# Sort comparisons by whole piece and chunk comparisons by whole load in a graph layer's scatter-add

## The chip, the cores and the metric

The kernel runs on one NeuronCore of one Trainium2 chip. The metric is device time in microseconds (us) of one execution. The core has five engines with a queue each: PE (TensorE, matrix products), DVE (VectorE), ACT (ScalarE), POOL (GpSimd, which here issues the indirect transfers) and SP (SyncE, which issues direct transfers). Each engine takes its instructions strictly in the order in which they stand in the program; an instruction that waits holds up all behind it on the same engine.

## The reference

`x` has 6250 nodes of 128 features, `edge_attr_128` has 206,250 edges of 128 features, and `src` names the node of each edge. What is computed:

```python
edge_aggr = zeros(n, 128).at[src].add(edge_attr_128)         # scatter-add of the edges
combined  = concat([x, edge_aggr, global_expand]) @ W_c + b_c
h = softplus(combined @ W1 + b1)
h = softplus(h @ W2 + b2)
out = layernorm(x + h @ W3 + b3)
```

Nearly all of the time goes into the scatter-add.

## The kernel before, in words

The nodes are cut into 32 **buckets** of 196 nodes. The edges lie in 1692 columns of 122 edges; two columns are a **pair** (846 pairs), three pairs a **piece** (`PAIRS`, 286 pieces with the short ones), and the pieces are cut into 8 groups. The scatter-add runs in three stages that overlap from beginning to end:

1. **Positions.** For each group `positions` works out, on DVE and PE by turns, at which place of its bucket each edge goes (DVE tiles `pair_ib`, `past`, `slot`, `pair` and many small ones). The result for sorting is `slot`: the place of each edge inside its column.
2. **Sort and scatter.** For each piece: *compare* makes 0/1 matrices (`sort_hot`, one 122x128 matrix for each column) out of `slot`; *gather* multiplies them on PE with the loaded edge rows, so that a column's rows come out sorted (`sorted`, three columns to a PSUM bank); *settle* copies them on ACT into one of six sets (`pairs`, line 1165); and POOL issues one indirect transfer for each pair (line 1182, `rows_by<-pairs,pair`), 846 in all, which puts the rows into their buckets in memory (`rows_by`).
3. **Chunks.** Rows come back bucket by bucket as **chunks** of 128 rows (1758 of them) in **loads** of at most eight chunks (`LOAD_CHUNKS`, 301 loads). *match* (line 983, DVE) compares the node of each row with the 196 nodes of the bucket (`hot`, 128x196 for each chunk), *product* (line 1006, PE) multiplies the chunk with that matrix and adds up in PSUM (`part`), and *add* (line 1029, DVE) adds a finished part to `sums_t`.

A piece has two **units**: its three even columns and its three odd ones. Before, the even unit is compared on DVE in one instruction over 3x128 elements (line 1133), and the odd unit on ACT, with three Abs instructions over 128 elements (line 1140) and one Relu over 384 (line 1142). A load's chunks are cut into units of at most `HALF` = 4 chunks: one match and one run of products each, 512 units in all.

The order on PE, DVE, ACT and SP is written out by a planner: every step is given a due time with `when(t, step)`, all steps are sorted by it, and each engine's instructions are issued in that order. The due times come from a model in which a pair is scattered every `SCATTER` = 1.3; for a piece that is scattered from t on, the compare is due at t - `COMPARED`, the gather at t - `GATHERED` and the settle at t - `SETTLED`. The due times are not times on the chip: they only set the order. In `sum_steps` a match is due no earlier than the product of the unit `TOGETHER` = 2 before it (`AT_END` before it, after the last scatter), and a load no earlier than the product that frees its buffer.

When the last pair is scattered, the steps left over are handed as `rest` to `node_layers`, which works through the chunks that remain and, as soon as the sums of a tile of nodes are there, runs the dense layers, the softplus and the layer norm on it: at each step up to `FIRST_STEPS` of the left-over steps, then the second and third products, then the rest that the next tile needs.

## Time and profile before

Times and the profiled execution:

| | |
|---|---|
| median of 3 runs | 1299.63 us (1296.0 to 1299.84) |
| the profiled execution's own time | 1298.25 us |
| its span, first to last instruction | 1296.5 us |
| mean granted TensorE clock | 0.963 |
| busy PE / DVE / ACT / POOL | 1169.6 / 1073.4 / 1064.2 / 877.7 us |
| scatters (POOL) | 846, the first issued at 23.4 us, the last at 1132.4 us |

What lies between the span and the profiled execution's time is 1.75 us. A row of a group of instructions names line, engine and operation, the tiles (out<-in), the shape, the count, then the busy time, the mean of one in ns, and the engine's idle time just before them with what ended it. A row of the timeline begins with the start in us and the duration; "x2" there is two instructions that follow each other without a gap, and what stands in brackets is the idle time before them and what ended it. A TensorE product of 32-bit numbers appears as two MATMULs and two weight loads, so 162 MATMULs on line 1006 are 81 chunks.

### The profile page before, as it was taken

The numbers are of one execution on the slowest core, as the hardware profiler recorded it, in microseconds if no ns is written. First come the engines' busy times: TensorE is split into PE (matmuls) and PEld (weight loads), VectorE is DVE, ScalarE is ACT, GpSimd is POOL, SyncE is SP. The second block draws the span as 40 slices with busy tenths as digits, with TensorE's granted clock in tenths as the row PEclk, the third lists the DMA queues.
The fourth block names the chain that finished last, engine by engine and source line by source line (L and its number), as shares of the span: only waits on it lengthen the run. The fifth ranks groups of instructions, "written<-read, shape, count | busy, mean of one in ns | idle before, by whom it ended". The sixth has DMA issues, their size and how long they took to land.

```text
span 1296.5 us, 26618 instructions
## 1 busy us (share of the span) xinstructions
PE 1169.6 (90%) x8617; PEld 1108.0 (85%) x8617; DVE 1073.4 (83%) x2403; ACT 1064.2 (82%) x2484; POOL 877.7 (68%) x915
## 2 busy tenths in 40 slices
PE   5767898878999998999899999999999999999893
PEld 4657788877998898998799999999999999998762
DVE  7968988998899988899878887799877666687784
ACT  5998998899978898987999999998999999504353
POOL 2777777777776677776777777777777777740334
PEclk9888998989999899999999999999999999999996
DMA  6789998899999998996989999999999999874421
GB/s 227 245 273 346 344 326 305 305 337 369 364 321 316 362 329 295 311 316 238 314 296 306 325 332 321 355 294 325 337 348 336 361 340 353 279 220 144 142 77 52
DMA packets 174638, 381.99 MB, mean 295 GB/s; under 512 B 27546, under 2 KB 118626, under 8 KB 160670
## 3 DMA queue, kind: packets, MB, share of 16 engines
q1 hardware_dynamic: 130751, 260.70, 60.4%
q0 software_dynamic: 41328, 115.65, 23.0%
q10 hardware_dynamic: 2415, 3.87, 0.8%
q8 instruction: 72, 1.18, 0.4%
q14 instruction: 72, 0.59, 0.1%
HBM read 242.49 MB, written 142.20 MB: 297 GB/s over the span
## 4 chain that ended last, share of the span: by engine, by line
PE 42%; DVE 21%; DMA 15%; ACT 9%; issue 7%; POOL 6%; SPq 0%; ACTq 0%; DVEq 0%; POOLq 0%
PE part L1006 24%; PE sorted L1153 13%; DMA rows_by<-pairs,pair 11%; POOL rows_by L1182 6%; ACT pairs L1165 6%; DVE hot L983 4%; DMA chunks<-rows_by 3%; ACT sort_hot L1140 2%; DVE sort_hot L1133 2%; DVE pair_ib L491 2%; DVE past L720 2%; DVE sums_t L1029 2%; DVE slot L569 1%; PE small L1383 1%; DMA rows<-in_edge 1%
## 5 line engine op out<-in xcount | busy, mean ns | idle before, releaser
L1182 POOL DMA_INDIRECT rows_by<-pairs,pair x846 | 824.8, 975 | 306.9 <-issue 204.5
L1006 PE MATMUL part<-hot,chunks 128*128 128x196 f32 x3516 | 674.1, 335 | 12.2 <-DVE sums_t L1029 9.2
L1165 ACT COPY pairs<-sorted 64x387 f32<-64x387 f32 (+2 forms) x1144 | 542.7, 474 | 70.0 <-PE sorted L1153 49.5
L1006 PEld LDWEIGHTS part<-hot,chunks 128*128 128x128 f32 x3516 | 581.1, 192 | 21.2 <-DVE sums_t L1029 10.3
L1153 PE MATMUL sorted<-rows,sort_hot 122*128 122x129 f32 x3384 | 497.4, 287 | 43.3 <-ACT pairs L1165 37.2
L1153 PEld LDWEIGHTS sorted<-rows,sort_hot 122*128 122x128 f32 x3384 | 454.0, 198 | 55.6 <-ACT pairs L1165 51.8
L983 DVE TENSOR_TENSOR hot<-chunks,both_ps 128x784 f32<-128x784 f32 (+3 forms) x541 | 427.9, 810 | 5.6 <-DMA chunks<-rows_by 5.2
L1140 ACT ACTIVATE sort_hot<-plain,slot 122x128 f32<-122x128 f32 x846 | 278.3, 391 | 13.1 <-DVE slot L569 7.1
L1029 DVE TENSOR_TENSOR sums_t<-sums_t,part 128x392 f32<-128x392 f32 (+1 forms) x262 | 143.5, 548 | 117.4 <-PE part L1006 116.7
L1142 ACT ACTIVATE sort_hot<-sort_hot,ones 122x384 f32<-122x384 f32 (+2 forms) x286 | 174.6, 611 | 9.3
L1133 DVE TENSOR_TENSOR sort_hot<-slot,both_ps 122x384 f32<-122x384 f32 (+2 forms) x286 | 154.5, 541 | 3.2 <-PE sorted L1153 3.0
L491 DVE TENSOR_TENSOR pair_ib<-pair_block,both_ps 122x512 bf16<-122x512 bf16 (+2 forms) x157 | 103.5, 664 | 0.3
L1425 POOL TENSOR_SCALAR y<-y,mv,rs 128x128 f32<-128x128 f32 x40 | 31.1, 785 | 96.9 <-issue 67.7
L569 DVE TENSOR_REDUCE slot<-small 122x16 f32<-122x512 f32 (+2 forms) x109 | 72.8, 668 | 15.3 <-PE small L552 14.8
L1355 ACT ACTIVATE away<-sorted,z_bias 128x512 f32<-128x512 f32 (+2 forms) x13 | 8.5, 656 | 70.8 <-DMA chunks<-rows_by 46.3
L550 PE MATMUL small<-pair_ib,half 122*122 122x512 bf16 (+2 forms) x109 | 43.0, 395 | 10.0 <-DVE slot L569 9.6
L735 PEld LDWEIGHTS <-past 128*128 128x128 f16 x424 | 24.9, 99 | 17.9 <-DVE past L720 12.6
L720 DVE TENSOR_TENSOR past<-both_ps,starts 128x512 f16<-128x512 f32 (+1 forms) x61 | 40.0, 666 | 0.3
L735 PE MATMUL small<-jump,past 128*128 128x56 f16 (+3 forms) x424 | 29.2, 190 | 11.5 <-DVE past L720 8.1
L1107 ACT COPY rows<-pair_i 122x16 f32<-122x16 f32 x106 | 22.6, 213 | 17.8 <-DMA rows<-in_edge 16.9
L552 PEld LDWEIGHTS <-starts_h 128*122 128x122 bf16 x236 | 24.9, 146 | 12.1 <-issue 7.6
L720 DVE TENSOR_TENSOR past<-both_ps,starts_late 128x512 f16<-128x512 f32 (+2 forms) x49 | 32.3, 661 | 0.0
(163 smaller groups left out, 520.0 us busy)
## 6 DMA issues: line engine op xcount, KB each, us to landing
rows<-in_edge SPq DMA_DIRECT2D x105, 1032.0 KB
chunks<-rows_by SPq DMA_DIRECT2D x362, 136.0 KB
chunks<-rows_by SPq DMA_DIRECT2D x203, 204.0 KB
chunks<-rows_by SPq DMA_DIRECT2D x75, 272.0 KB
rows_by<-pairs,pair POOLq DMA_INDIRECT x846
rows_by<-fill SPq DMA_DIRECT2D x10, 1249.5 KB
rows_by<-fill SPq DMA_DIRECT2D x10, 714.0 KB
chunks<-rows_by SPq DMA_DIRECT2D x13, 408.0 KB
```

Of the source, the lines that this page charges most:

```text
L491: nc.vector.tensor_tensor(ib, pair_block[:, cols].unsqueeze(2).to_broadcast([PN, n, SB]), iota_ps[:PN, :SB].unsqueeze(1).to_broadcast([PN, ...
L569: nc.vector.tensor_reduce(to, of, axis=mybir.AxisListType.X, op=ALU.max)
L720: nc.vector.tensor_tensor(past[:, :, a:b], twice_ps[:KB].unsqueeze(1).unsqueeze(1).to_broadcast([KB, 2, b - a, P // 2]), own["starts"][:, ...
L983: nc.vector.tensor_tensor(hot[:, q - a:q - a + m], chunks[j][:, lo:hi + 1:step, D:W].to_broadcast([P, m, BL]), iota_ps.unsqueeze(1).to_bro ...
L1006: nc.tensor.matmul(part[:, b - base_of[v], :], t[:, place_in(j, q), :D], hot[:, q - a], start=first, stop=last)
L1029: nc.vector.tensor_add(here, here, of)
L1133: nc.vector.tensor_tensor(hot[:PN, :m], slot[:PN, at:at + 2 * m - 1:2].unsqueeze(2).to_broadcast([PN, m, P]), slot_ps[:PN].unsqueeze(1).to ...
L1140: nc.scalar.activation(hot[:PN, j], by_slot[:PN], AF.Abs, bias=slot[:PN, at:at + 1], scale=-1.0)
L1142: nc.scalar.activation(hot[:PN, :m], hot[:PN, :m], AF.Relu, bias=ones[:PN, :1], scale=-1.0)
L1153: nc.tensor.matmul(out[:, j, :], hot[:PN, j], rows_at[col // LOAD_COLS][:PN, col % LOAD_COLS, :], start=True, stop=True)
L1165: nc.scalar.copy(sets_at[i][64 * n:64 * n + 64, lo:lo + m, h, :W], out[64 * h:64 * h + 64, :m, :])
L1182: s = nc.gpsimd.indirect_dma_start(out=dst, out_offset=bass.IndirectOffsetOnAxis(ap=at, axis=0), in_=rows[:, j].rearrange("p a b -> p (a b ...
```

## The change

It has four parts.

- **Sort comparisons by piece.** `compare` takes a whole piece, six columns. Even pieces are compared on DVE, in one instruction over 6x128 elements; odd pieces on ACT, in six Abs over 128 elements and one Relu over 768. On ACT the seven instructions are seven steps with due times of their own, 0.65 apart (`SCATTER` / 2) and beginning `SPREAD` = 2.0 earlier, so that settles of earlier pieces come to stand between them. The tile `sort_hot` is twice as large, and there are three in place of five.
- **Chunks by whole load.** `HALF` goes from 4 to 8: a load is one unit. There are 301 units in place of 512; three `hot` tiles of eight chunks stand in place of six of four.
- **The end.** `AT_END` goes from 4 to 2 units and `FIRST_STEPS` from 9 to 5 steps.
- The bias of the Relu and of the logarithm is the constant 1.0 in place of a column of the tile `ones`.

```diff
-HALF = 4
+HALF = 8
...
-SHARE = 2
+SHARE, SPREAD = 2, 2.0
 PREP, LAG = 0.85, 11.0
 TOGETHER, BEHIND = 2, 1
-AT_END, FIRST_STEPS = 4, 9
+AT_END, FIRST_STEPS = 2, 5
...
-    hots = ctx.enter_context(tc.tile_pool(name="hots", bufs=6))
+    hots = ctx.enter_context(tc.tile_pool(name="hots", bufs=3))
...
-        sort_p = phase.enter_context(tc.tile_pool(name="sort", bufs=5))
+        sort_p = phase.enter_context(tc.tile_pool(name="sort", bufs=3))
...
-        def compare(unit):
-            i, lo, m, n = unit
-            g, c, _ = pieces[i]
-            slot = slot_of[g]
...
-            hot = sort_p.tile([P, THREE, P], F32, name="sort_hot")
-            hot_of[unit] = hot
-            if (2 * i + n) % SHARE == 0:
-                at = 2 * (c - groups[g][0] + lo) + n
-                nc.vector.tensor_tensor(
-                    hot[:PN, :m],
-                    slot[:PN, at:at + 2 * m - 1:2].unsqueeze(2).to_broadcast([PN, m, P]),
-                    slot_ps[:PN].unsqueeze(1).to_broadcast([PN, m, P]), op=ALU.is_equal)
-                return
-            for j in range(m):
-                at = 2 * (c - groups[g][0] + lo + j) + n
-                nc.scalar.activation(hot[:PN, j], by_slot[:PN], AF.Abs,
-                                     bias=slot[:PN, at:at + 1], scale=-1.0)
-            nc.scalar.activation(hot[:PN, :m], hot[:PN, :m], AF.Relu, bias=ones[:PN, :1],
-                                 scale=-1.0)
+        def compare(i):
+            g, c, m = pieces[i]
+            slot, at = slot_of[g], 2 * (c - groups[g][0])
...
+            hot = hot_of[i] = sort_p.tile([P, 2 * PAIRS, P], F32, name="sort_hot")
+            if i % SHARE == 0:
+                return [lambda: nc.vector.tensor_tensor(
+                    hot[:PN, :2 * m], slot[:PN, at:at + 2 * m].unsqueeze(2).to_broadcast([PN, 2 * m, P]),
+                    slot_ps[:PN].unsqueeze(1).to_broadcast([PN, 2 * m, P]), op=ALU.is_equal)]
+            return [lambda j=j: nc.scalar.activation(
+                hot[:PN, j], by_slot[:PN], AF.Abs, bias=slot[:PN, at + j:at + j + 1], scale=-1.0)
+                for j in range(2 * m)] + [lambda: nc.scalar.activation(
+                    hot[:PN, :2 * m], hot[:PN, :2 * m], AF.Relu, bias=1.0, scale=-1.0)]
...
-                nc.tensor.matmul(out[:, j, :], hot[:PN, j],
+                nc.tensor.matmul(out[:, j, :], hot[:PN, at],
...
+            comparing = {}
+
+            def compare_next(i):
+                if i not in comparing:
+                    comparing[i] = compare(i)
+                comparing[i].pop(0)()
+
             for i, t in enumerate(begins):
                 mine = units(i)
+                soon = 0.0 if i else SOON
+                if i % SHARE == 0:
+                    when(t - COMPARED - soon, lambda i=i: compare_next(i))
+                else:
+                    for j in range(2 * pieces[i][2] + 1):
+                        when(t - COMPARED - SPREAD + j * SCATTER / 2, lambda i=i: compare_next(i))
                 for u, unit in enumerate(mine):
...
-                    when(t - COMPARED + late_by - soon, lambda unit=unit: compare(unit))
...
-            nc.scalar.activation(away[:, :w], away[:, :w], AF.Ln, bias=ones[:, :1])
+            nc.scalar.activation(away[:, :w], away[:, :w], AF.Ln, bias=1.0)
```

In the built program the DVE instructions of line 983 go from 541 to 346, the DVE sort comparisons from 286 to 143, the Relus from 286 to 143 and the Abs from 846 to 840; PE's products, the copies, the scatters and all transfers keep their number.

Three places show how the order moves. The first is DVE while the second half of the sixth group's positions is made (`pair_ib`, `past`, `slot`); before:

```order
L1029 TENSOR_TENSOR sums_t<-sums_t,part 128x392
L983 TENSOR_TENSOR hot<-chunks,both_ps 128x588
L1133 TENSOR_TENSOR sort_hot<-slot,both_ps 122x384
L491 TENSOR_TENSOR pair_ib<-pair_block,both_ps 122x512
L983 TENSOR_TENSOR hot<-chunks,both_ps 128x588
L720 TENSOR_TENSOR past<-both_ps,starts_late 128x512
L569 TENSOR_REDUCE slot<-small 122x2x2x4
```

and with the change:

```order
L1029 TENSOR_TENSOR sums_t<-sums_t,part 128x392
L983 TENSOR_TENSOR hot<-chunks,both_ps 128x1176
L1130 TENSOR_TENSOR sort_hot<-slot,both_ps 122x768
L491 TENSOR_TENSOR pair_ib<-pair_block,both_ps 122x512
L693 TENSOR_TENSOR earlier_late<-earlier_late 128x64
L696 SCALAR_TENSOR_TENSOR far<-plain 128x1
```

Two matches of three chunks have become one of six, and the sort comparison is twice as wide; in the next cycle of DVE, not shown, there is none.

The second place is ACT in the middle of the program; `pairs_112` and `pairs_113` are the sets of two pieces that follow each other. Before:

```order
L1140 ACTIVATE sort_hot<-plain,slot 122x128 x3
L1142 ACTIVATE sort_hot<-sort_hot,ones 122x384
L1165 COPY pairs_112<-sorted 64x3x129 x4
L1140 ACTIVATE sort_hot<-plain,slot 122x128 x3
L1142 ACTIVATE sort_hot<-sort_hot,ones 122x384
L1165 COPY pairs_113<-sorted 64x3x129 x4
```

and with the change:

```order
L1158 COPY pairs_112<-sorted 64x3x129 x4
L1133 ACTIVATE sort_hot<-plain,slot 122x128 x2
L1158 COPY pairs_113<-sorted 64x3x129 x2
L1133 ACTIVATE sort_hot<-plain,slot 122x128 x3
L1158 COPY pairs_113<-sorted 64x3x129 x2
L1133 ACTIVATE sort_hot<-plain,slot 122x128
L1135 ACTIVATE sort_hot<-sort_hot 122x768
```

The comparison of one odd piece now stands between the copies of two pieces, and the four copies of the second of them are split by three Abs.

The third place is PE in the last group, between gathers (line 1153, now 1146) and products (line 1006). Before:

```order
L1153 MATMUL sorted<-rows,sort_hot 128x129 x3
L1006 MATMUL part<-hot,chunks 128x196 x3
L1153 MATMUL sorted<-rows,sort_hot 128x129 x3
L1006 MATMUL part<-hot,chunks 128x196 x3
L1153 MATMUL sorted<-rows,sort_hot 128x129 x3
```

and with the change:

```order
L1146 MATMUL sorted<-rows,sort_hot 128x129 x3
L1006 MATMUL part<-hot,chunks 128x196 x6
L1146 MATMUL sorted<-rows,sort_hot 128x129 x6
L1006 MATMUL part<-hot,chunks 128x196 x6
L1146 MATMUL sorted<-rows,sort_hot 128x129 x6
```

Gathers of three columns and products of three chunks used to alternate; now both units of a piece are gathered in one go, and a whole load is multiplied in one go.

More of the change, by code (lines that the diff above doesn't have):

```diff
@@ L1122 @@
         hot_of, sorted_of = {}, {}
[L1124 to L1143 removed]
+        def compare(i):
+            g, c, m = pieces[i]
+            slot, at = slot_of[g], 2 * (c - groups[g][0])
+            assert all((g, at + j) in slots_done for j in range(2 * m))
+            hot = hot_of[i] = sort_p.tile([P, 2 * PAIRS, P], F32, name="sort_hot")
[7 more added lines that the diff above has]
+                    hot[:PN, :2 * m], hot[:PN, :2 * m], AF.Relu, bias=1.0, scale=-1.0)]
         def gather(unit):
             i, lo, m, n = unit
[L1147 removed]
+            hot = hot_of[i]
             out = opened_bank(lambda: settle(unit))
```

2 lines of the change are left out of this document (removed).

## The prediction

> **What bounds the kernel now.** I read the scatters first, since everything after them waits for the last one. This is line 1182 by itself, and two rows of POOL's timeline in a quiet place:
>
> ```profile
> L1182 POOL DMA_INDIRECT rows_by<-pairs,pair x846: 971/972/1222, 23.4 to 1132.4; - x170
> ...
> 1000.81 0.97 POOL L1182 DMA_INDIRECT rows_by<-pairs,pair  x1 [0.30 <-issue]
> 1002.09 0.97 POOL L1182 DMA_INDIRECT rows_by<-pairs,pair  x1 [0.30 <-issue]
> ```
>
> Undisturbed, a scatter starts 1.28 us after the one before (1002.09 - 1000.81; 0.97 busy and 0.30 of issue). 845 such steps are about 1080 us; from 23.4 to 1132.4 the kernel took 1109. So only some **29 us** of the scatter stage are lateness; nothing in the change touches the 1.28. Where they lie is seen by stage, with the busy time and count of each engine:
>
> ```profile
> core 0: us, PE busy (x) PEld busy (x) DVE busy (x) ACT busy (x) POOL busy (x), PEclk, DMA share, GB/s
> 120.00:320.00 200.00, 171.63 (x1373) 160.66 (x1372) 176.78 (x433) 181.04 (x429) 149.50 (x154) 0.94 0.91 325
> 320.00:640.00 320.00, 296.97 (x2340) 285.95 (x2339) 292.66 (x677) 278.12 (x658) 228.42 (x235) 0.97 0.90 317
> 640.00:1120.00 480.00, 474.50 (x3478) 467.53 (x3477) 377.51 (x671) 450.02 (x1064) 363.21 (x374) 0.99 0.94 326
> 1133.00:1297.00 164.00, 132.01 (x672) 110.41 (x672) 119.14 (x286) 55.21 (x95) 52.19 (x65) 0.92 0.43 129
> ...
> 565.00:621.00 56.00, 50.67 (x401) 47.70 (x400) 55.49 (x128) 44.23 (x106) 37.76 (x40) 0.97 0.80 287
> ```
>
> From 320 to 640 POOL issued 235 scatters, 300 us' worth, in 320: **about 20 of the 29 us** are there, 3 between 120 and 320 (154 are 197), about 1 after 640 (374 are 478). What POOL and the engines behind it waited for from 320 to 640 (total us, times, longest):
>
> ```profile
> ACT pairs L1165 <- PE sorted L1153: 21.0, 24, 2.6
> POOL rows_by L1182 <- ACT pairs L1165: 18.8, 19, 3.6
> ACT rows L1107 <- DMA rows<-in_edge: 10.9, 4, 3.9
> POOL rows_by L1182 <- DMA rows_by<-pairs,pair: 8.9, 19, 1.9
> DVE z_bias L1079 <- PE small L1078: 4.8, 1, 4.8
> ```
>
> POOL waits for ACT's copies, ACT for PE's gathers, and PE for DVE, as the timeline of DVE in the fullest stretch shows (565 to 621, DVE busy 55.49 of 56 us):
>
> ```profile
> 577.64 0.75 DVE L983 TENSOR_TENSOR hot<-chunks,both_ps 128x588 f32<-128x588 f32 x1
> 578.32 0.54 DVE L1133 TENSOR_TENSOR sort_hot<-slot,both_ps 122x384 f32<-122x384 f32 x1
> 578.78 0.68 DVE L491 TENSOR_TENSOR pair_ib<-pair_block,both_ps 122x512 bf16<-122x512 bf16 x1
> ...
> 582.40 0.54 DVE L1133 TENSOR_TENSOR sort_hot<-slot,both_ps 122x384 f32<-122x384 f32 x1
> ...
> 585.81 0.96 DVE L983 TENSOR_TENSOR hot<-chunks,both_ps 128x784 f32<-128x784 f32 x1
> 586.69 0.54 DVE L1133 TENSOR_TENSOR sort_hot<-slot,both_ps 122x384 f32<-122x384 f32 x1
> ```
>
> There is one `sort_hot` per piece, so DVE's cycle is 582.40 - 578.32 = **4.08 us a piece**, against 3 x 1.28 = 3.83 for its three scatters: 0.25 us late with every piece. DVE leads in such stretches; elsewhere in 320 to 640 it is transfers (the third to fifth rows of the waits). From 640 on PE is busy 474.5 of 480 us while POOL keeps its pace, so there a faster DVE or ACT buys nothing.
>
> **The change, part by part. DVE's merged comparisons.** The matches fall from 541 to 346 instructions, the sort comparisons from 286 to 143; the elements stay. A merge saves what an instruction costs beside its elements. By duration:
>
> ```profile
> L983 DVE TENSOR_TENSOR hot<-chunks,both_ps 128x784 f32<-128x784 f32 x230 | 218.9, 963 | 5.3 <-DMA chunks<-rows_by 5.0
> L983 DVE TENSOR_TENSOR hot<-chunks,both_ps 128x588 f32<-128x588 f32 x223 | 166.7, 759 | 0.3 <-DMA chunks<-rows_by 0.2
> L983 DVE TENSOR_TENSOR hot<-chunks,both_ps 128x392 f32<-128x392 f32 x81 | 42.6, 554 | 0.0
> ```
>
> 784 - 392 elements cost 409 ns, 1.04 ns each; 588 x 1.04 = 612, and 759 - 612 leaves **0.147 us** fixed. But from start to start the 588 above took 578.32 - 577.64 = 0.68 us and the 784 took 0.88: 588 x 1.04 leaves **0.068**, 784 leaves 0.065. The next instruction begins before the last has ended, so in a stretch without gaps a merge saves 0.065. I take 0.065, since only full stretches matter, and keep 0.147 as the upper end. In all 338 merges are 22 us of DVE (50 by duration), most of it where DVE has time anyway. [...]
>
> In the full stretch two pieces lose three instructions (two matches of three become one of six twice, two sort comparisons become one): 3 x 0.065 = 0.195 us, **0.10 a piece of the 0.25 that are late**, two fifths. If all 20 us of 320 to 640 were DVE's that is 8 us; with the 10.9, 8.9 (of which 19 x 0.30 are ordinary issue) and 4.8 us of transfer and PE waits in it, I take 0.4 x 15 = **-6**. Bounds: 0 (PE busy 297 of 320 does not let it through) and 0.147 x 3 / 2 = 0.22 a piece, 0.88 x 20 = -17.6.
>
> **ACT.** Its parts, by shape:
>
> ```profile
> L1165 ACT COPY pairs<-sorted 64x387 f32<-64x387 f32 x1116 | 534.5, 479 | 68.0 <-PE sorted L1153 48.0 <-PE small L552 0.2 <-DMA rows_by<-pairs,pair 0.2
> L1140 ACT ACTIVATE sort_hot<-plain,slot 122x128 f32<-122x128 f32 x846 | 278.3, 391 | 13.1 <-DVE slot L569 7.1
> L1142 ACT ACTIVATE sort_hot<-sort_hot,ones 122x384 f32<-122x384 f32 x279 | 171.6, 615 | 9.0
> L1142 ACT ACTIVATE sort_hot<-sort_hot,ones 122x128 f32<-122x128 f32 x5 | 2.0, 401 | 0.2
> ```
>
> Two pieces take 8 x 0.479 + 6 x 0.391 + 2 x 0.615 = 7.41 us of the 7.67 in which they are scattered: ACT is nearly full and, once late, regains 0.26 per two pieces. The Relu costs (615 - 401) / 256 = 0.84 ns an element and 0.29 fixed, so one over 768 elements is 0.94 in place of 1.23: 7.12, and it regains 0.55, twice as fast. This can only shorten lateness that outlasts its cause; the 3 us of 120 to 320 and what is left of 320 to 640 are of that kind. I take **-1.5** (0 to -5). Moving the steps costs nothing by itself: between the last copies of an even and of an odd piece ACT now has two Abs, two copies, three Abs, two copies, 5 x 0.391 + 4 x 0.479 = 3.87 us, and from there to the next even piece one Abs, the Relu and four copies, 3.25; 3.87 is 0.04 over the pace. If the copies lead by less than that, it is 0.04 once.
>
> **Start.** The first piece is compared on DVE as a whole: 384 elements more, 0.40 us, ahead of the first gather. I take **+0.4** (0 to 0.4; its odd half leaves ACT).
>
> **After the last scatter.** PE does the chunks that are left and the dense layers, and is held up in places:
>
> ```profile
> 1134.94 0.97 DVE L983 TENSOR_TENSOR hot<-chunks,both_ps 128x784 f32<-128x784 f32 x1 [2.52 <-DMA chunks<-rows_by]
> ...
> 1136.44 28.81 PE L1006 MATMUL part<-hot,chunks 128*128 128x196 f32 x162 [3.51 <-DVE sums_t L1029]
> ...
> 1202.28 1.56 PE L1006 MATMUL part<-hot,chunks 128*128 128x196 f32 x8 [1.68 <-issue]
> ...
> 1218.79 1.59 PE L1006 MATMUL part<-hot,chunks 128*128 128x196 f32 x8 [1.02 <-DVE sums_t L1029]
> ...
> 1246.65 1.59 PE L1006 MATMUL part<-hot,chunks 128*128 128x196 f32 x8 [1.22 <-DVE sums_t L1029]
> ```
>
> The 3.51 us are the wait for the last rows: the load lands, DVE compares four chunks (0.97), adds, and PE goes on. Eight chunks are 4 x 196 x 1.04 = 0.82 us more, on the path: **+0.8**. From the last sort comparison on 93 matches become 64, which spares DVE 29 x 0.065 = 1.9 us (4.3 at 0.147), and DVE is what the other rows wait for; against it a match of 1.7 us can stand ahead of an add. `AT_END` halved over units twice as long keeps the same look-ahead in chunks, and five steps for nine likewise. I take **-1.0** (-4 to +4). A trade that the stretch of DVE decides either way.
>
> The bias of 1.0 is an operand in another place: nothing, since no instruction is added. Three `hot` tiles of eight hold as many chunks as six of four, but a load of two chunks takes a whole one; where DVE is ahead of PE, in the 640 to 1120 in which it is busy only 377.51 of 480 us, a wait for a tile costs nothing that the wait of an add for the same products does not: 0, or, where DVE leads, a part of the bound of 0 for its gain.
>
> **Sum:** -6 - 1.5 + 0.4 + 0.8 - 1.0 = **-7.3 us**. From the profiled execution's 1298.25 that is 1291.0. The median of the runs, 1299.63, lies 0.1% above that execution, within their spread of 3.8 us; I stay with **1291**.
>
> **The rivals.** *The whole fixed cost comes back.* If every merge in the full stretches spares 0.147 us, 0.22 of the 0.25 a piece go, 17.6 us in place of 6, and the lateness ends almost wholly: 1298.25 - 17.6 - 1.3 = 1279. For it: the rows by duration; against it: the starts. [...] Chance 0.12.
>
> *No change.* PE decides. It is busy 297 of 320 us before 640 and without a gap after, and its work is the same. To end 7 us sooner it must lose 7 of the 23 idle us in that stage; if these are its waits for loads (10.9 us on ACT's side) and not for DVE, POOL's gain is eaten by PE's, and 1296 to 1301 comes out. For it: 474.5 of 480; against it: in the full stretch, 565 to 621, the waits run from PE to DVE. Chance 0.24.
>
> *Slower: longer runs of products ahead of the gathers.* PE now runs six to eight chunks in one go where three or four stood between two gathers. A chunk is 28.81 / 81 = 0.36 us, so a gather behind it can come 3 x 0.36 = 1.07 us later, and its copies and scatters too, where nothing is in hand. Over the whole run:
>
> ```profile
> POOL rows_by L1182 <- ACT pairs L1165: 30.0, 40, 3.6
> ```
>
> 40 times POOL already waits for the copies. If the longer run comes on top at 15 of them, that is +16, with the -7.3 about 1307; it decides from about 11 places on (11 x 1.07 = 11.8, the gain and 0.3%). Against it: both units of a piece are now gathered together, so the wait comes once a piece. Chance 0.16.
>
> **How the numbers follow.** Below 0.3%, 3.9 us, this kernel's measurement can't tell a change. The forecast has 0.48, by itself 1285 to 1295.7; with the first rival, faster is 0.60; the same 0.24; slower 0.16. The range takes in the bound of 17.6 us for DVE with a little more from ACT, 1277, and of the slower case what lies near, 1303: beyond them I leave about 0.06 and 0.13.
>
> **What would show it.** Right: the matches of 1568 elements take 1.78 us (0.147 + 1.63) and the sort comparisons of 768 take 0.95; the Relu 0.94; the last scatter starts near 1125 in place of 1132; the scatters from 320 to 640 rise from 235 to about 240; in the full stretch DVE's cycle falls to about 8.0 us for two pieces; POOL's waits for ACT's copies fall. The time from the last scatter to the end stays within 3 us of 164. Wrong: POOL's waits for copies grow, or the gathers wait for the Relu (the slower case); the last scatter comes sooner but the tail grows by as much (PE decides); or DVE begins to wait at line 983 for PE, which means that three tiles are too few.

## The result: 0.5% slower, and the profile after

The changed kernel takes 1304.12 us (median of 12 executions, 1302.13 to 1311.17), the kernel before, measured beside it, 1298.91 (12 executions, 1296.0 to 1300.53). The ratio is **1.0052, 95% interval 1.0035 to 1.0068**: 5.2 us slower, where 1291 had been forecast with a range up to 1303. The profiled execution took 1303.65 us with a span of 1301.9.

The page and the view of the scatters' line show that the work per engine fell as it should, and that the scatters nevertheless ended later:

```profile
PE 1168.6 (90%) x8617; PEld 1111.4 (85%) x8617; DVE 1051.6 (81%) x2065; ACT 1003.2 (77%) x2335; POOL 878.9 (68%) x915
```

```profile
L1175 POOL DMA_INDIRECT rows_by<-pairs,pair x846: 971/972/1417, 23.5 to 1137.6; - x170
```

DVE is busy 22 us less than before, ACT 61 us less. The first scatter starts at 23.5 (before 23.4), the last at 1137.6 (before 1132.4). From there to the end are 1301.9 - 1137.6 = 164.3 us (before 1296.5 - 1132.4 = 164.1). So in these two profiles the whole loss lies between the first and the last scatter, and the two constants of the end have hardly a part in it. By stage (columns as in the same view of before):

```profile
120.00:320.00 200.00, 170.42 (x1387) 160.28 (x1387) 176.83 (x398) 171.98 (x406) 150.08 (x153) 0.96 0.92 326
320.00:640.00 320.00, 291.67 (x2280) 282.73 (x2280) 279.69 (x562) 253.84 (x597) 224.75 (x230) 0.95 0.89 311
640.00:1120.00 480.00, 474.97 (x3492) 469.16 (x3491) 371.44 (x520) 427.09 (x1005) 364.35 (x375) 1.00 0.95 327
```

From 120 to 320 and from 640 on the count of scatters is within one of what it was. From 320 to 640 POOL issued 230 in place of 235, 5 x 1.28 = 6.4 us' worth less, although DVE was busy 13 us less there. Part of that is the five scatters that are missing; for each scatter DVE was busy 279.69 / 230 = 1.216 us in place of 292.66 / 235 = 1.245, which is 6.9 us over 235. **DVE's saving is there, and the scatters did not get it.** The waits that answer to those of the prediction, over the whole run:

```profile
ACT pairs L1158 <- PE sorted L1146: 122.8, 125, 6.2
...
POOL rows_by L1175 <- ACT pairs L1158: 44.0, 64, 4.9
...
PE sorted L1146 <- ACT sort_hot L1135: 25.9, 19, 2.2
...
DVE hot L983 <- PE part L1006: 9.6, 11, 2.2
```

POOL's waits for the copies grew from 30.0 us in 40 to 44.0 in 64, and the longest from 3.6 to 4.9. Gathers now wait for the Relu (25.9 us), and DVE for a `hot` tile (9.6 us). These are the signs that the prediction named for being wrong: longer waits for copies, gathers that wait for the Relu, DVE that waits for a tile. ACT's wait for gathers, 122.8 us where it was 49.5, is no such sign: with the sort part alone, which does not lose (next section), it is 109.7.

### The profile page after: what moved, and what is told of

It is laid out like the page before. It is cut to its first block, busy times and chain, and to the rows that moved or that the text cites. A ratio compares the mean times of both kernels' runs of the same rounds, so it can differ in the third digit from the quotient of the medians.

```text
span 1301.9 us, 26116 instructions
## 1 busy us (share of the span) xinstructions
PE 1168.6 (90%) x8617; PEld 1111.4 (85%) x8617; DVE 1051.6 (81%) x2065; ACT 1003.2 (77%) x2335; POOL 878.9 (68%) x915
## 4 chain that ended last, share of the span: by engine, by line
PE 58%; DVE 19%; DMA 11%; ACT 7%; issue 4%; POOL 1%; SPq 0%; DVEq 0%; ACTq 0%; POOLq 0%
PE part L1006 34%; PE sorted L1146 18%; DMA chunks<-rows_by 5%; DVE hot L983 4%; ACT pairs L1158 4%; DMA rows_by<-pairs,pair 3%; ACT sort_hot L1133 2%; DVE pair_ib L491 2%; DVE sort_hot L1130 2%; DVE slot L569 2%; DVE past L720 1%; DMA rows<-in_edge 1%; DVE sums_t L1029 1%; PE small L550 1%; PE small L552 1%
## 5 line engine op out<-in xcount | busy, mean ns | idle before, releaser
L1006 PE MATMUL part<-hot,chunks 128*128 128x196 f32 x3516 | 648.4, 336 | 21.6 <-DVE sums_t L1029 10.5
L1158 ACT COPY pairs<-sorted 64x387 f32<-64x387 f32 (+2 forms) x1144 | 542.6, 474 | 141.7 <-PE sorted L1146 122.8
L1006 PEld LDWEIGHTS part<-hot,chunks 128*128 128x128 f32 x3516 | 588.7, 193 | 32.2 <-DVE sums_t L1029 12.2
L1146 PE MATMUL sorted<-rows,sort_hot 122*128 122x129 f32 x3384 | 479.0, 286 | 42.2 <-ACT sort_hot L1135 25.9
L1146 PEld LDWEIGHTS sorted<-rows,sort_hot 122*128 122x128 f32 x3384 | 438.1, 197 | 51.2 <-ACT sort_hot L1135 29.5
L983 DVE TENSOR_TENSOR hot<-chunks,both_ps 128x1568 f32<-128x1568 f32 (+7 forms) x346 | 404.5, 1185 | 22.5 <-DMA chunks<-rows_by 10.8
L1133 ACT ACTIVATE sort_hot<-plain,slot 122x128 f32<-122x128 f32 x840 | 292.8, 394 | 18.0 <-DVE slot L569 7.0
L1130 DVE TENSOR_TENSOR sort_hot<-slot,both_ps 122x768 f32<-122x768 f32 x143 | 134.5, 941 | 6.7 <-PE sorted L1146 6.5
L1135 ACT ACTIVATE sort_hot<-sort_hot 122x768 f32<-122x768 f32 x143 | 118.6, 830 | 3.9
L502 PE MATMUL small<-ones_h,pair_ib 122*128 122x48 bf16 x423 | 18.7, 190 | 14.8 <-DVE pair_ib L491 14.3
```

Of the source, the lines that this page charges most:

```text
L983: nc.vector.tensor_tensor(hot[:, q - a:q - a + m], chunks[j][:, lo:hi + 1:step, D:W].to_broadcast([P, m, BL]), iota_ps.unsqueeze(1).to_bro ...
L1006: nc.tensor.matmul(part[:, b - base_of[v], :], t[:, place_in(j, q), :D], hot[:, q - a], start=first, stop=last)
L1130: return [lambda: nc.vector.tensor_tensor(hot[:PN, :2 * m], slot[:PN, at:at + 2 * m].unsqueeze(2).to_broadcast([PN, 2 * m, P]), slot_ps[:P ...
L1133: return [lambda j=j: nc.scalar.activation(hot[:PN, j], by_slot[:PN], AF.Abs, bias=slot[:PN, at + j:at + j + 1], scale=-1.0) for j in rang ...
L1135: for j in range(2 * m)] + [lambda: nc.scalar.activation(hot[:PN, :2 * m], hot[:PN, :2 * m], AF.Relu, bias=1.0, scale=-1.0)]
L1146: nc.tensor.matmul(out[:, j, :], hot[:PN, at], rows_at[col // LOAD_COLS][:PN, col % LOAD_COLS, :], start=True, stop=True)
```

## The experiments

### Which part loses: the sort part alone, and the whole loads alone

Theory A: the whole loads lose; a match of eight chunks and a run of eight products stand in one piece in the order of DVE and PE, and what the next scatters need stands behind them. Theory B: the sort part loses; the last of ACT's seven steps comes late, and the gathers of odd pieces wait for the Relu.

`sort_only`, the changed kernel with these lines as before:

```diff
-HALF = 8
+HALF = 4
-AT_END, FIRST_STEPS = 2, 5
+AT_END, FIRST_STEPS = 4, 9
-    hots = ctx.enter_context(tc.tile_pool(name="hots", bufs=3))
+    hots = ctx.enter_context(tc.tile_pool(name="hots", bufs=6))
```

> Only the sort comparisons by piece (even pieces on VectorE, odd ones in short steps on ScalarE); chunk units stay at four, six hot tiles, AT_END 4, FIRST_STEPS 9. Theory A (the loss comes from whole loads: matches of up to 1.78 us and runs of up to eight products stand ahead of what the scatters need): without them the sort part gains a little, 1293 to 1298 us, ratio 0.995 to 0.999, last scatter at 1127 to 1132. Theory B (the loss comes from the sort part: both gathers of an odd piece now wait for the last Relu on ScalarE, 25.9 us of PE's waits in the changed kernel): the loss is all here, 1302 to 1306 us, last scatter near 1138.

`load_only`, the kernel before with those three lines as in the change ("whole loads" below means all three, the constants of the end with them):

> Only the whole loads (HALF 8, three hot tiles of eight, AT_END 2, FIRST_STEPS 5); the sort comparisons are those of before. Theory A: the loss is all here or more, 1303 to 1309 us, and ScalarE's wait for PE's gathers lies well over the 49.5 us of before. Theory B: 1295 to 1300 us, no loss.

Measured against the kernel before on one chip (1297.39 us, 17 executions): `sort_only` 1295.98 us, **0.9982 [0.9966, 0.9998]**; `load_only` 1312.43 us, **1.0108 [1.0089, 1.0127]**. In `load_only`'s profile the last scatter starts at 1142.0; the time lies above the 1303 to 1309 that theory A gave it. The whole loads lose, and the sort part gains a little: theory A holds. The two do not add to the changed kernel (0.9982 and 1.0108 would be 1.009, and it is 1.0052); on the sort part the whole loads cost less than on the comparisons of before.

`spread4` asks theory B directly: the changed kernel with ACT's steps due 2.0 earlier.

```diff
-SHARE, SPREAD = 2, 2.0
+SHARE, SPREAD = 2, 4.0
```

> The changed kernel with SPREAD 4.0 in place of 2.0: ScalarE's comparison of an odd piece is due 2.0 sooner. Theory B: PE's wait for the last Relu falls from 25.9 us to under 10 and the time to 1298 to 1301 us. Theory A: the wait may fall, the time stays at 1302 to 1306.

It takes 1305.31 us, 1.0066 [1.005, 1.0083], on the chip of the two runs above. The waits for the Relu, 25.9 us in the changed kernel, are gone from its list, but nothing is won: the wait moved to DVE's side, which now waits for one of the three `sort_hot` tiles:

```profile
DVE sort_hot L1130 <- PE sorted L1146: 66.3, 44, 4.4
```

`sort_only` has the Relu waits too (26.3 us) and is no slower than before. Theory B falls, and with it the second of the prediction's signs: the wait for the Relu is no mark of the slower case.

### Where the whole loads lose it

The four longest waits of a scatter for ACT's copies from 438 on in the changed kernel's profile, and then the waits at the same places with the sort part alone (in brackets the wait; 0.30 of it is usual):

```profile
444.08 0.97 POOL L1175 DMA_INDIRECT rows_by<-pairs,pair  x1 [4.90 <-ACT pairs L1158]
...
508.42 0.97 POOL L1175 DMA_INDIRECT rows_by<-pairs,pair  x1 [3.84 <-ACT pairs L1158]
...
583.61 0.97 POOL L1175 DMA_INDIRECT rows_by<-pairs,pair  x1 [2.46 <-ACT pairs L1158]
...
606.30 0.97 POOL L1175 DMA_INDIRECT rows_by<-pairs,pair  x1 [2.86 <-ACT pairs L1158]
```

```profile
442.45 0.97 POOL L1175 DMA_INDIRECT rows_by<-pairs,pair  x1 [2.35 <-ACT pairs L1158]
...
503.48 0.97 POOL L1175 DMA_INDIRECT rows_by<-pairs,pair  x1 [1.47 <-ACT pairs L1158]
...
582.27 0.97 POOL L1175 DMA_INDIRECT rows_by<-pairs,pair  x1 [1.41 <-ACT pairs L1158]
...
601.24 0.97 POOL L1175 DMA_INDIRECT rows_by<-pairs,pair  x1 [1.81 <-ACT pairs L1158]
```

At the four places together the changed kernel waits 14.06 us and the sort part 7.04. A second profiled execution of each, taken later (`after_again` and `sort_only2` below), has the same places: 4.94, 3.84, 2.46 and 2.85 for the changed kernel (14.09), 3.63, 1.47, 1.41 and 1.81 for the sort part (8.32). So 5.8 to 7.0 us come from four places that recur, and most of it from the first two.

The starts of the scatters say the same without a choice of rows. From the 301st scatter, at about 421 us, to the last it is 716.3 and 716.4 us in the two profiles of the changed kernel, 710.0 and 710.7 in those of the sort part, and 711.2 in the kernel before: some 6 us. Up to the 301st the profiles differ by a few us either way, those of one kernel too.

What stands in front of the first one, on DVE and PE; the changed kernel first:

```profile
433.36 0.95 DVE L1130 TENSOR_TENSOR sort_hot<-slot,both_ps 122x768 f32<-122x768 f32 x1
...
435.42 3.28 DVE L983 TENSOR_TENSOR hot<-chunks,both_ps 128x1568 f32<-128x1568 f32 x2
```

```profile
434.46 1.63 PE L1146 MATMUL sorted<-rows,sort_hot 122*128 122x129 f32 x6 [3.82 <-DVE sort_hot L1130]
437.26 4.87 PE L1006 MATMUL part<-hot,chunks 128*128 128x196 f32 x16 [1.17 <-DVE hot L983]
441.97 0.83 PE L1146 MATMUL sorted<-rows,sort_hot 122*128 122x129 f32 x6
```

and the sort part alone:

```profile
433.82 0.95 DVE L1130 TENSOR_TENSOR sort_hot<-slot,both_ps 122x768 f32<-122x768 f32 x1
...
435.88 1.84 DVE L983 TENSOR_TENSOR hot<-chunks,both_ps 128x784 f32<-128x784 f32 x2
```

```profile
434.92 1.13 PE L1146 MATMUL sorted<-rows,sort_hot 122*128 122x129 f32 x6 [3.87 <-ACT sort_hot L1133]
436.90 2.98 PE L1006 MATMUL part<-hot,chunks 128*128 128x196 f32 x8 [0.86 <-DVE hot L983]
439.67 1.50 PE L1146 MATMUL sorted<-rows,sort_hot 122*128 122x129 f32 x6
```

Both stand at the start of a group, where DVE works on the group's pair numbers for some 5 us (not shown) and PE has nothing to do for 3.8. Then comes the comparison of a piece, a match, a run of products, and behind that run the gather for which ACT and POOL wait. From the start of the piece's comparison to that gather it is 441.97 - 433.36 = 8.61 us in the changed kernel and 439.67 - 433.82 = 5.85 in the sort part: **2.76 us more, of which 1.89 are the run of products** (4.87 for eight chunks, 2.98 for four); most of the rest is the longer match that the run waits for. And the run is slow: the clock granted to PE there (the column before the last two) was

```profile
437.00:442.00 5.00, 4.74 (x17) 4.74 (x18) 4.45 (x6) 0.10 (x1) 1.88 (x2) 0.57 0.99 335
```

0.57. 16 MATMULs at 4.87 us are 0.30 each, where the same 16 take 2.87, 0.18 each, in the fourth place below. The sort part's run goes at 2.98 / 8 = 0.37 each: the slow stretch is there in both, and the changed kernel has more work in it. The second place (changed kernel, then sort part) is of the same kind (the view ends at 506, before the sixteenth MATMUL of the changed kernel's run starts):

```profile
495.86 0.83 PE L1146 MATMUL sorted<-rows,sort_hot 122*128 122x129 f32 x6
501.10 5.20 PE L1006 MATMUL part<-hot,chunks 128*128 128x196 f32 x15 [4.41 <-DVE sums_t L1029]
...
506.31 1.50 PE L1146 MATMUL sorted<-rows,sort_hot 122*128 122x129 f32 x12
```

```profile
497.93 2.98 PE L1006 MATMUL part<-hot,chunks 128*128 128x196 f32 x8 [3.70 <-DVE sums_t L1029]
500.70 1.50 PE L1146 MATMUL sorted<-rows,sort_hot 122*128 122x129 f32 x6
```

From the end of the idle time to the gather: 5.21 us with eight chunks ahead of it, 2.77 with four, 2.44 more; the scatter waited 3.84 - 1.47 = 2.37 more. Against the sort part the longer run explains all of it here. The fourth place, in the full stretch, has both halves of the change in one chain:

```profile
595.93 3.27 DVE L983 TENSOR_TENSOR hot<-chunks,both_ps 128x1568 f32<-128x1568 f32 x2
599.12 0.68 DVE L569 TENSOR_REDUCE slot<-small 122x16 f32<-122x512 f32 x1
```

```profile
599.86 0.38 PE L550 MATMUL small<-pair_ib,half 122*122 122x512 bf16 x1 [2.23 <-DVE slot L569]
600.08 0.39 PE L552 MATMUL small<-half,starts_h_late 128*122 128x128 bf16 x4
600.30 2.87 PE L1006 MATMUL part<-hot,chunks 128*128 128x196 f32 x16
603.01 0.27 PE L735 MATMUL small<-jump,past 128*128 128x56 f16 x4
603.12 1.58 PE L1146 MATMUL sorted<-rows,sort_hot 122*128 122x129 f32 x12
```

Two long matches, 3.19 us from start to start of the next, stand in front of the position step `slot`; PE waits 2.23 us for it, and then runs eight chunks, at 0.18 us a MATMUL, before the gathers for which the scatter of 606.30 waits. The third place was not taken apart.

### Taking the two halves of it apart

`half_products`: the changed kernel with the products of a load of more than four chunks as two steps with due times of their own, while scatters run; the matches stay whole.

```diff
+            if e - a > 4 and at <= ends[-1]:
+                half = (e - a) // 2
+                found.append((product_at[n], len(found), lambda n=n, half=half: product(n, 0, half)))
+                found.append((product_at[n] + half * RATE, len(found), lambda n=n, half=half: product(n, half)))
```

> The changed kernel, with the products of a load of five to eight chunks issued as two steps of at most four, as long as scatters run; matches stay whole. Theory A, if it is the runs of products on PE that delay the gathers: 1296 to 1300 us, and the longest waits of ScalarE for a gather fall from 6.2 us to under 4. Theory A, if it is the wide matches on VectorE in front of position steps: 1302 to 1305, unchanged. Theory B: unchanged, 1302 to 1306.

1313.66 us, 1.0127 [1.0107, 1.0146]: worse than the changed kernel, and outside all that was expected. It does not separate the two, since the second half now comes later and holds the `hot` tile until then:

```profile
DVE hot L983 <- PE part L1007: 110.0, 98, 4.0
```

That wait was 9.6 us in the changed kernel. So three tiles are too few where something holds them longer; how much of the 9.5 us against the changed kernel that makes was not measured.

`wide_match` and `long_runs` therefore start from the sort part and keep its plan in units of four. `wide_match` writes the whole load's match at the due time of its first unit, into three tiles of eight; PE multiplies in runs of four:

```diff
+                if a:
+                    return
-                hot = hots.tile([P, HALF, BL], F32, name="hot")
-                hots_of[n] = hot
-                q = a
+                hot = hots.tile([P, LOAD_CHUNKS, BL], F32, name="hot")
+                hots_of[j] = hot
+                q, e = 0, len(loads[j][3])
```

`long_runs` keeps matches of four and six tiles, and writes all products of a load at the due time of its last unit:

```diff
-                j, a, e = units_of[n]
+                j, _, e = units_of[n]
+                if n != last_unit[j]:
+                    return
+                a = 0
```

> The kernel with the sort part alone (units of four), in which VectorE compares a whole load in one instruction at the due time of the load's first unit, into three hot tiles of eight; PE's order of products and gathers stays that of units of four. Theory A1 (the wide matches in front of position steps, which PE waits for, and the three tiles make the loss of the load part): 1304 to 1310 us, near the sort part's 1296 plus the load part's 8 to 13. Theory A2 (the long runs of products in front of gathers make it): 1293 to 1298 us, near the sort part alone.

> The kernel with the sort part alone (matches of at most four, six hot tiles of four), in which PE multiplies a whole load in one run at the due time of its last unit. Theory A2: 1304 to 1310 us, and ScalarE's longest wait for a gather rises from 4.2 to over 5 us. Theory A1: 1293 to 1299 us.

These two, and two repeats of them, ran on three chips on which the kernel before itself took 1593.52, 1595.11 and 1597.74 us (see the last section), so only their ratios count: `wide_match` 1.0094, 1.011 and 1.0111, `long_runs` 1.01, 1.0095 and 1.0104, all with intervals of some 0.4% to either side. Each half costs there, but the sort part had not been timed beside them, only a variant of it on the first of the three chips (`sort_deep` below, 0.9991). What was expected of the repeats:

> The sort part with whole loads in the comparisons alone (one instruction of up to eight chunks at the time of the load's first half, three tiles; products in runs of four). On a chip where the kernel before takes about 1298 us. If long comparisons in front of VectorE's position steps are what costs: 1.005 to 1.01 of the kernel before, last scatter 5 to 10 us later than 1132.4, and the later scatters follow position steps of VectorE (ScalarE's waits for gathered rows not above the 110 us of the sort part). If only the long TensorE runs cost: 0.998, last scatter within 2 us of 1132.4.

> The sort part with whole loads in the products alone (one run of up to eight chunks at the time of the load's last half; comparisons of at most four chunks, six tiles). On a chip where the kernel before takes about 1298 us. If long TensorE runs in front of gathers and position steps are what costs: 1.005 to 1.01, last scatter 5 to 10 us later than 1132.4, ScalarE's waits for gathered rows above the 110 us of the sort part. If only the long comparisons cost: 0.998, last scatter within 2 us of 1132.4. If both have a part: 1.002 to 1.006 in each of the two kernels.

The whole table then came from one chip on which the kernel before took 1298.87 us (27 executions):

> The sort part alone, for a table on one chip with the next three. Where the kernel before takes about 1298 us: 0.998, as measured. Where it takes about 1596 us: 0.997 to 1.000 by the theory that the sort part is a small gain everywhere; 1.005 or more if the losses of the single halves on such chips came from the sort part.

> The sort part and whole loads in the comparisons alone. Where the kernel before takes about 1298 us: 1.005 to 1.01 if the long comparisons cost, 0.998 if not. Where it takes about 1596 us: about 1.010 again; what of it is the halves' own is the difference from the sort part alone on the same chip.

> The sort part and whole loads in the products alone. Where the kernel before takes about 1298 us: 1.005 to 1.01 if the long runs cost, 0.998 if not. Where it takes about 1596 us: about 1.010 again, and the difference from the sort part alone is the half's own.

> The changed kernel. Where the kernel before takes about 1298 us: 1.005 as measured. Where it takes about 1596 us: about 1.010 if one cause (a whole load at one place in an engine's order) stands behind both halves, so that the second half adds little to the first; about 1.02 if they are two costs that add.

| on one chip | median us | against the kernel before |
|---|---|---|
| sort part alone (`sort_only2`) | 1294.26 | 0.9967 [0.9953, 0.9981] |
| with long matches (`wide_match4`) | 1296.96 | 0.9992 [0.9977, 1.0006] |
| with long runs of products (`long_runs4`) | 1297.89 | 0.9996 [0.9984, 1.0008] |
| with both, the changed kernel (`after_again`) | 1304.88 | 1.0050 [1.0030, 1.0070] |

By the ratios the long matches add 0.25% to the sort part and the long runs 0.29% (by the medians 2.7 and 3.6 us), **each less than expected of a cause that stands alone, and each hardly beyond its noise**, some 0.2% either way. The whole loads together add 0.83% (10.6 us), well clear of it. The profile of `long_runs4` has its own late place: a run of six chunks, after idle times of 1.34 and 1.53 us, took 3.77 us in front of the gathers for which a scatter waited 3.49:

```profile
577.91 0.38 PE L550 MATMUL small<-pair_ib,half 122*122 122x512 bf16 x1 [1.34 <-DVE jump L702]
578.12 0.39 PE L552 MATMUL small<-half,starts_h_late 128*122 128x128 bf16 x4
580.04 0.26 PE L735 MATMUL small<-jump,past 128*128 128x56 f16 x4 [1.53 <-DVE slot L569]
580.14 3.77 PE L1012 MATMUL part<-hot,chunks 128*128 128x196 f32 x12
583.71 1.69 PE L1152 MATMUL sorted<-rows,sort_hot 122*128 122x129 f32 x12
```

```profile
586.00 0.97 POOL L1181 DMA_INDIRECT rows_by<-pairs,pair  x1 [3.49 <-ACT pairs L1164]
```

The profiles of single executions cannot give the sizes: that of `wide_match4` is the fastest execution of its kernel (1293.96 us, with the last scatter at 1126.0, sooner than before) and that of `sort_only2` the slowest (1299.58), so the medians stand for the sizes and the profiles for the places.

For the places the profiles say more. From the 301st scatter to the last it is 709.5 us with long matches alone and 712.0 with long runs alone, one profile each, against 710.0 and 710.7 with neither and 716.3 and 716.4 with both. So the 6 us located above hardly show with either half alone. (A single wait can mislead: with long matches alone the scatter at the first place waits 4.20 us, and yet this stretch is no longer.) At the second place `long_runs4` has the same long run after an idle time:

```profile
497.14 1.86 PE L1152 MATMUL sorted<-rows,sort_hot 122*128 122x129 f32 x12
501.55 4.60 PE L1012 MATMUL part<-hot,chunks 128*128 128x196 f32 x16 [2.55 <-DVE sums_t L1035]
```

and yet from 495 to 508 no scatter waits more than 0.31. Ahead of the idle time stand the gathers of six columns (x12), where the changed kernel has those of three (495.86, x6). A long run by itself is not enough, then; it costs where the order puts it ahead of gathers that are due. Where the 2.7 and 3.6 us of the single halves lie is open.

`both_own_times` asks whether the missing 0.3% (0.83 against 0.25 + 0.29) comes of the plan in units of eight, which also sets a match two whole loads ahead of its product. It is `wide_match` and `long_runs` in one kernel, at the due times of units of four:

> Long comparisons and long runs together as in the changed kernel, but at the due times that the plan of units of four gave them (the comparison at that of the load's first half, the run at that of its last half), where the changed kernel plans in units of eight (comparison two whole loads ahead of its product). On one chip the sort part alone measured 0.9967, with long comparisons 0.9992, with long runs 0.9996, and the changed kernel 1.005. If the two costs simply add: 0.9967 + 0.0025 + 0.0029 = 1.002, and the rest of the change's loss, 0.003, is the plan in units of eight. If each makes the other dearer: 1.004 to 1.006, as the changed kernel. Where the kernel before takes about 1596 us, only a ratio of about 1.02 against about 1.01 would tell the same.

1.0142 [1.0103, 1.0181], on a chip where the kernel before took 1590.95 us: more than either half on such chips (about 1.010), less than both would add if the sort part gained nothing there. That does not settle it; and with intervals of 0.12 to 0.2% for each ratio of the table, the difference of 0.3% is itself at the edge of the noise. The profiles from the 301st scatter on speak for a loss that needs both halves or the plan in units of eight; which of these stays open.

### Two attempts to do better

Both ran on chips of the slower kind. `sort_deep` gives the sort part four `sort_hot` tiles (five `hot` tiles to make room) and `SPREAD` = 3.5, against its Relu waits:

> The kernel with the sort part alone, with four sort_hot tiles in place of three, five hot tiles in place of six, and SPREAD 3.5: ScalarE's comparison of an odd piece is due 1.5 sooner. If PE's waits for the last Relu (26.3 us with the sort part alone) still cost scatters, they fall under 10 us and the time to 1289 to 1294 us. If those waits lie where PE has time in hand, the waits fall and the time stays at 1293 to 1298 us.

0.9991 [0.9959, 1.0023], no gain that can be told. `units_of_two` cuts the sort part's units at two chunks, with twelve tiles and the same look-ahead in chunks:

```diff
-HALF = 4
+HALF = 2
-TOGETHER, BEHIND = 2, 1
-AT_END, FIRST_STEPS = 4, 9
+TOGETHER, BEHIND = 4, 2
+AT_END, FIRST_STEPS = 8, 17
```

> The sort part with units cut at two chunks instead of four, twelve tiles, and as many chunks of lookahead as before: the change of the unit in the other direction. If size of unit works in both directions (granularity): last scatter 2 to 6 us earlier than 1132.4, ratio 0.993 to 0.997. If VectorE's fixed cost per instruction weighs more (0.065 us for each of some 200 further instructions, in stretches where VectorE leads): last scatter 3 to 6 us later, 1.001 to 1.004. If the loss at eight comes only of a limit that four does not reach: 0.998 as with the sort part alone.

1.0147 [1.0108, 1.0187]: on that chip shorter units lose as well, and more than either long half (1.011 and 1.0095 there). `one_ahead`, the changed kernel with `TOGETHER` = 1, so that a match stands one unit of eight ahead of its product:

> The changed kernel with a unit compared one unit ahead of its product instead of two, so that as many chunks lie between the comparison and the product as before the change (eight, not sixteen). If the loss comes of comparing too early (VectorE does work that is not yet needed in front of position steps, and three tiles are all held): 0.999 to 1.002 of the kernel before. If it comes of the long pieces themselves: 1.004 to 1.007 as the changed kernel, or more, since TensorE then waits for the comparisons.

1.0215 [1.0162, 1.0268] on the same chip, where the changed kernel itself was not timed; nothing speaks for matches that come too early. The best version remains the sort part alone: 0.9982 and 0.9967 of the kernel before, measured twice on one chip, 2 to 4 us; on another chip it may differ.

## Why the prediction was wrong, point by point

- **What bounds the kernel**: right. In the profiles all of the difference lies in the scatter stage, and there from 320 to 640.
- **"0.10 a piece of the 0.25 that are late" and the -6 made of it**: this is the step that failed. The saving was sized rightly as work (0.10 a piece of three scatters is 0.033 a scatter; DVE's busy time fell by 0.029 a scatter), but it was counted as time won wherever scatters were late. What is late is the one result that stands behind a long instruction or a long run in the order of an engine, and two merges of three were bought with just that. These two, -4 of the -6, measured +10.6 us on the sort part.
- **"Three hot tiles ... 0"** and the silence of the sum on longer runs: the whole loads belonged in it with a positive term. They cost +1.08% on the kernel before and 0.83% on the sort part: by the medians 2.7 us for long matches, 3.6 for long runs, and some 4 more for both together with their plan. DVE's wait for a tile, put at 0, came to 9.6 us; what it cost is not shown.
- **The slower rival** had one half of the mechanism: longer runs of products ahead of gathers. Its price, 1.07 us a place, is three further chunks at 0.36 us, from a stretch in which PE was granted 0.94 of its clock. At the two group starts there are four, 1.43 us at that price, and they cost 1.89 and 2.44, where PE was granted 0.57 of its clock from 437 to 442 and 0.50 from 501 to 506. Its "point from which it decides", eleven places, was therefore too far off: four places carried 5.8 to 7.0 us. That its 1307 lies near the 1304 measured is in part luck: the price was too small and the places too many. The other half, matches of 1.6 to 1.8 us ahead of the position steps, was named only for the end. Its counter-argument (both units of a piece are gathered together, so the wait comes once) held no comfort: at the first place the run stands between the two units of one piece (gathers at 434.46 and 441.97), and one wait of 4.90 us loses as much as two short ones.
- **ACT -1.5, and what the sort comparisons gave of the -6**: right in sign and size; the mechanism is not shown. By the prediction's own terms the sort part alone is one merge of three (-2), -1.5 and +0.4, about -3; it measured -2.3 and -4.3 us (0.9982 and 0.9967 of the medians of before). But in its two profiles the last scatter starts at 1132.3 and 1134.7, no sooner than the 1132.4 of before, so that the gain is not seen in the stage for which it was forecast, and the agreement may be luck. "Moving the ACT steps costs nothing" stands: its Relu waits are there and cost nothing that shows.
- **Start +0.4, end -0.2**: the first scatter came 0.1 us later, the time after the last scatter is 164.3 against 164.1; right.
- **Durations of merged instructions**: by shape,

```profile
L983 DVE TENSOR_TENSOR hot<-chunks,both_ps 128x1568 f32<-128x1568 f32 x85 | 151.0, 1782 | 13.7 <-DMA chunks<-rows_by 7.0 <-PE part L1006 6.6
...
L1130 DVE TENSOR_TENSOR sort_hot<-slot,both_ps 122x768 f32<-122x768 f32 x141 | 133.4, 946 | 4.2 <-PE sorted L1146 4.0
L1135 ACT ACTIVATE sort_hot<-sort_hot 122x768 f32<-122x768 f32 x138 | 116.3, 843 | 3.9
```

  1.78 and 0.95 us as forecast; the Relu takes 0.84 where 0.94 was forecast.
- **"The bias of 1.0 ... nothing"**: wrong, though not what failed. The Relu over 256 elements, with the column of `ones` (line 1142) and with the constant (line 1135):

```profile
L1142 ACT ACTIVATE sort_hot<-sort_hot,ones 122x256 f32<-122x256 f32 x2 | 1.0, 508 | 0.1
L1135 ACT ACTIVATE sort_hot<-sort_hot 122x256 f32<-122x256 f32 x4 | 1.7, 413 | 0.0
```

  The constant makes an instruction 95 ns shorter. With it, 256 to 768 elements cost (843 - 413) / 512 = 0.84 ns each, as before; the fixed part fell from 0.29 to 0.20 us. That is the 0.1 us by which the Relu beat its forecast, some 14 us of ACT over 143 of them; what it did to the time was not measured by itself.

## What to carry to other kernels

Before instructions are merged on an engine, look at what stands right behind them in its order and who waits for it: the gain is a fixed cost per merge (0.065 us from start to start here), the price is up to the whole added length at every place where the result behind is late (2.76 and 2.44 us at the two group starts). The place decides: behind the same long run no scatter waited more than 0.31 us where a whole piece had been gathered ahead of it. Price a TensorE run by the clock that the trace shows where it stands (0.57 and 0.50 at the two group starts), and not by the mean of the span (0.963). And split a change that has two independent parts: here the one gained 0.2 to 0.3% and the other took 0.8% to 1.1%.

## What the runs showed of the hardware that I had not expected

**TensorE's clock after idle time.** After 3.82 and 1.17 us of idle time the run at 437.26 went at 0.30 us a MATMUL, after 4.41 us the run at 501.10 at 0.35, after 2.23 us the run at 600.30 at 0.18. I knew the granted clock only as a mean (0.963 before and after), which hides that it was 1.00 from 429 to 434, 0.57 from 434 to 442 and 0.50 from 501 to 506, and scatters were late behind both of these runs; from 600 to 603 it was 1.00. The run at 580.14 in `long_runs4` above took 0.31 us a MATMUL after idle times of 1.34 and 1.53 us (granted clock 0.58 from 580 to 584), where the run of twelve at 573.47, ahead of them, took 2.15 us, 0.18 each. So the length of the last idle time alone does not tell the clock: 1.53 us stood before 0.58, 2.23 before 1.00. That the idle time brings the clock down is my reading of these places; no run was made to show it.

**Chips differ by more than any change here.** On four chips the kernel before took 1591 to 1598 us, where in the comparison with the change and on the chip of the other tables it took 1297 to 1299. PE's own products take hardly longer there, 350 ns where the profile of the kernel before has 335, but PE stands idle without a cause that the profile shows (47.3 us on this line, where that of before has 1.7). Against the same kernel on the other chip (`wide_match4`) PE's mean granted clock is 0.900 in place of 0.967, and POOL waits ten times as long for copies (309.4 us in place of 30.4). These are the rows of `wide_match2`, a repeat of `wide_match`:

```profile
L1177 POOL DMA_INDIRECT rows_by<-pairs,pair x846 | 824.1, 974 | 606.5 <-ACT pairs L1160 309.4 <-issue 218.6 <-ACT rows L1109 42.6
L1008 PE MATMUL part<-hot,chunks 128*128 128x196 f32 x3516 | 726.8, 350 | 64.3 <-issue 47.3 <-DVE hot L985 6.9 <-PE part L1008 3.1
```

On that chip scatters are late in every stretch (118 from 120 to 320, 191 from 320 to 640 and 188 from 640 to 960, where the profile of the kernel before has 154, 235 and 249), and on three of the four chips the kernels with one long half take about 1% more than the kernel before, where they took 0.9992 and 0.9996 of it on the other. What makes PE stand still there was not found.
